# A two-layer graph kernel: one sum per feed-forward unit, and twelve sums of features, moved between ScalarE, GpSimd and VectorE

## The chip, the cores and the metric

The kernel runs on one core of one Trainium2 chip. The metric is the device time of one launch in microseconds (us), taken from repeated runs of the same program. Beside it stands a profile of one execution, which names what each engine did and when. The engines are called as the profile calls them: PE is TensorE (the matrix multiplier; PEld is its weight load), DVE is VectorE, ACT is ScalarE, POOL is GpSimd, and SP is SyncE, which here only issues transfers. Every engine works through its own list of instructions strictly in order; where one needs the result of another engine, it waits for a semaphore, and everything behind it in the same list waits too.

## The reference, cut to what matters

The input is 128 graphs of 128 nodes with 256 features each, and an integer adjacency matrix per graph. Two layers follow one another. All of it is float32.

```python
# layer 0: graph attention twice, then a feed-forward network
h = _gat(x, adj, W1, a1);  h = _gat(h, adj, W2, a2)     # softmax over masked scores
h = _layernorm(x + h, g_ln1, b_ln1)
x = _layernorm(h + relu(h @ w_ff1 + b_ff1) @ w_ff2 + b_ff2, g_ln2, b_ln2)

# layer 1: 8-head attention with 4 relations, then a feed-forward network
attn = softmax(q @ k.T / sqrt(32))
out  = sum over r of (attn * (adj == r)) @ (x @ Wv[r])
x = _ln(x + out @ Wo, g1, beta1)
x = _ln(x + gelu(x @ W1 + b1) @ W2 + b2, g2, beta2)
```

The change touches the first product of each feed-forward network, `h @ w_ff1` and `x @ W1`: for a group of 4 graphs it is a 512 x 256 matrix times a 256 x 1024 matrix.

## The kernel before

The graphs are worked through in 32 groups of 4. For each group there are stages (loading, graph attention, feed-forward of layer 0, multi-head attention, feed-forward of layer 1), written as Python generators. A small scheduler in the kernel interleaves the stages of neighbouring groups by planned times; for most of the kernel it also pins the order in which PE and SP get their instructions. The order on DVE, ACT and POOL comes out of the compiler's own scheduling, and it is fixed when the program is built.

The feed-forward product is done by a scheme of the Strassen kind: both matrices are cut into 2 x 2 blocks, and 7 block products and some sums of blocks take the place of 8 products. The sums of the weights are made once. The sums of the features are made once for each group and layer:

```python
def moving_sums(hT):                                        # line 279
    b11, b21, b12, b22 = ...                                # four blocks of the transposed features
    t1, t2, t4 = ...                                        # tiles of 128 x 256
    nc.gpsimd.tensor_sub(t1, b12, b11)                      # L283
    nc.gpsimd.tensor_sub(t2, b22, t1)                       # L284
    nc.gpsimd.tensor_sub(b12, b22, b12)                     # L285
    nc.gpsimd.tensor_sub(t4, t2, b21)                       # L286
    return None, b11, b21, b22, t4, t1, t2, b12
```

The results are made in two units for each group and layer, so there are 2 x 2 x 32 = 128 units in the kernel, and the two of one group take turns. One unit goes through four steps, and between the steps the other unit and other stages have their turn:

```python
def unit(f0):
    # lo, hi: two tiles of 128 x 2 x 2 x 256 in SBUF
    def product(p, k, first=False):                         # two matmuls of 256 columns
        for i in range(2):
            nc.tensor.matmul(p[:, i], win[k][...], hs[k], start=first and i == 0, stop=True, ...)  # L307

    chain, side = (ps.tile([P, 2, T // 2], F32, name="mm") for _ in range(2))   # PSUM
    product(chain, 1, True)
    product(side, 5, True)
    nc.scalar.copy(lo[:, :, 0], chain)                      # L313
    nc.scalar.copy(hi[:, :, 0], side)                       # L314
    yield
    p = ps.tile([P, 2, T // 2], F32, name="mm")
    product(chain, 6)
    product(p, 2, True)
    product(side, 3)
    nc.scalar.copy(lo[:, :, 1], chain)                      # L320
    nc.vector.tensor_add(lo[:, :, 0], lo[:, :, 0], p)       # L321
    nc.vector.tensor_add(lo[:, :, 1], lo[:, :, 1], side)    # L322
    yield
    product(chain, 7)
    nc.scalar.copy(hi[:, :, 1], chain)                      # L325
    nc.gpsimd.tensor_add(hi[:, :, 1], hi[:, :, 1], hi[:, :, 0])   # L326
    for i in range(2):
        nc.scalar.activation(lo[:, i], lo[:, i], func, ...) # L328
    yield
    product(chain, 4)
    for h, p in enumerate((chain, hi[:, :, 1])):
        for i in range(2):
            nc.scalar.activation(hi[:, i, h], p[:, i], func, ...)  # L334
    yield
```

Note the two products on `chain` at the end. Product 7 is added to `chain`; then that state of `chain` must be read out before product 4 is added on top of it. So the matmuls of product 4 wait for whoever reads `chain` after product 7.

Other lines that matter below, by their numbers in the profile:

```python
nc.gpsimd.tensor_tensor(y[...], y[...], v[...], op)         # L245 affine: gain and offset of a layer norm
nc.scalar.activation(y[:, b], y[:, b], AF.Identity, ...)    # L239 layer norm
nc.tensor.transpose(...)   /   nc.scalar.copy, nc.vector.tensor_copy   # L256, L260, L258: features on PE
nc.vector.transpose(z, y)                                   # L262: features by way of transfers
nc.tensor.matmul(..., fT[f][...], wout[:, f], ...)          # L351: second product of the feed-forward
nc.vector.tensor_add(y[...], y[...], p)                     # L352: and its sum with the residual
nc.scalar.copy(wh[...], p)                                  # L407, after the matmuls L406 (graph attention)
nc.tensor.matmul(scores...)                                 # L450
nc.vector.scalar_tensor_tensor(m, ab, r, eT, ...)           # L476: mask of one relation, four of them per graph
nc.tensor.matmul(p, hT..., wv...)  /  nc.vector.tensor_add(v..., p, bv)   # L483, L484: values
nc.tensor.matmul(po..., v..., ms[r]...)                     # L495: attention times values
```

PSUM holds six tiles named `mm` in turn for nearly all matmuls. The features reach their transposed form in two ways: for most groups by a DVE transpose of blocks and two transfers through DRAM, but for the first and the last group (`direct`) by PE, because nothing else could hide the transfers there.

Of the kernel before, what the change touches and what calls it, by code (L numbers as in the profile page):

```python
# [57 lines left out]
def graph_layers(ctx: ExitStack, tc: tile.TileContext, a: dict, out: bass.AP):  # L58
# [8 lines left out]
    nc = tc.nc  # L67
# [156 lines left out]
    def normalised(y, first=0, n=G):  # L224

        y = y[:, first:first + n]
        mv = sm.tile([P, n, 2], F32, name="mv")
        for b in range(n):
            st = sm.tile([P, 6], F32, name="st")
            nc.vector.bn_stats(st, y[:, b])  # L230
            nc.vector.bn_aggr(mv[:, b], st)
        rstd = sm.tile([P, n], F32, name="rstd")
        nc.gpsimd.tensor_scalar(rstd, mv[:, :, 1], EPS, None, op0=OP.add)
        nmr = sm.tile([P, n], F32, name="nmr")
        nc.gpsimd.tensor_scalar(nmr, mv[:, :, 0], -1.0, None, op0=OP.mult)
        nc.gpsimd.tensor_tensor(rstd, rstd, mhalf[:, :n], OP.pow)
        nc.gpsimd.tensor_mul(nmr, nmr, rstd)  # L237
        for b in range(n):
            nc.scalar.activation(y[:, b], y[:, b], AF.Identity, bias=nmr[:, b:b + 1], scale=rstd[:, b:b + 1])  # L239

    def affine(y, k, b, n, engine=nc.gpsimd):


        for op, v in zip((OP.mult, OP.add), ln[k]):
            engine.tensor_tensor(y[:, b:b + n], y[:, b:b + n], v[:, None, :].to_broadcast([P, n, D]), op)  # L245
# [26 lines left out]
    def features(y, direct):  # L272

        t = t_tile().rearrange("p (b c n) -> p b c n", b=G, c=DC)
        blocks = t.rearrange("p b c n -> p (b c) n")
        transposed(y.rearrange("p b (c f) -> p (b c) f", f=P), blocks, direct, blocks)
        return t

    def moving_sums(hT):

        b11, b21, b12, b22 = (hT[:, h:h + G // 2, c] for h in (0, G // 2) for c in range(DC))
        t1, t2, t4 = (wk.tile([P, G // 2, N], F32, name=f"t{i}") for i in (1, 2, 4))
        nc.gpsimd.tensor_sub(t1, b12, b11)  # L283
        nc.gpsimd.tensor_sub(t2, b22, t1)  # L284
        nc.gpsimd.tensor_sub(b12, b22, b12)  # L285
        nc.gpsimd.tensor_sub(t4, t2, b21)  # L286
        return None, b11, b21, b22, t4, t1, t2, b12

    def feed_forward(y, before, direct, win, bin_, wout, func, by=G):


        hT = features(y, direct)
        yield TIMES["lead ff0" if before == "01" else "lead ff1"]
        hs = moving_sums(hT)
        yield TIMES["sums"]
        fT = [None] * FC

        def unit(f0):

            lo, hi = (wk.tile([P, 2, 2, T // 2], F32, name="fT", bufs=FC // 2) for _ in range(2))  # L300
            for i in range(2):
                fT[f0 + i] = lo[:, i].rearrange("p h t -> p (h t)")
                fT[FC // 2 + f0 + i] = hi[:, i].rearrange("p h t -> p (h t)")

            def product(p, k, first=False):
                for i in range(2):
                    nc.tensor.matmul(p[:, i], win[k][:, ts(f0 + i, P)], hs[k], start=first and i == 0, stop=True,  # L307
                                     skip_group_check=True)

            chain, side = (ps.tile([P, 2, T // 2], F32, name="mm") for _ in range(2))  # L310
            product(chain, 1, True)
            product(side, 5, True)
            nc.scalar.copy(lo[:, :, 0], chain)  # L313
            nc.scalar.copy(hi[:, :, 0], side)  # L314
            yield
            p = ps.tile([P, 2, T // 2], F32, name="mm")
            product(chain, 6)
# [4 lines that stand above are left out]
            nc.vector.tensor_add(lo[:, :, 1], lo[:, :, 1], side)  # L322
            yield
            product(chain, 7)
            nc.scalar.copy(hi[:, :, 1], chain)  # L325
            nc.gpsimd.tensor_add(hi[:, :, 1], hi[:, :, 1], hi[:, :, 0])  # L326
            for i in range(2):
                nc.scalar.activation(lo[:, i], lo[:, i], func, bias=bin_[:, f0 + i:f0 + i + 1])  # L328
            yield
# [3 lines that stand above are left out]
                    f = FC // 2 + f0 + i  # L333
                    nc.scalar.activation(hi[:, i, h], p[:, i], func, bias=bin_[:, f:f + 1])  # L334
            yield

        units = [unit(0), unit(2)]
        for n, now in enumerate(((0,), (1,), (0,), (1,), (0,), (1,), (0,), (1,))):
            for u in now:
                next(units[u])  # L340
            if n in (2, 4):
                affine(y, before, n - 2, 2)
            yield TIMES["ff unit"]
        yield TIMES["ff2"]

        late = sorted(range(FC), key=lambda f: f % (FC // 2) // 2)
        for b2_ in range(0, G, 2):
            p = ps.tile([P, 2, D], F32, name="mm")
            for b in (b2_, b2_ + 1):
                for n, f in enumerate(late):  # L350
                    nc.tensor.matmul(p[:, b - b2_], fT[f][:, ts(b, N)], wout[:, f], start=n == 0, stop=n == FC - 1)  # L351
            nc.vector.tensor_add(y[:, b2_:b2_ + 2], y[:, b2_:b2_ + 2], p)  # L352
            yield TIMES["ff half"]
            if (b2_ + 2) % by == 0:
                normalised(y, b2_ + 2 - by, by)
        return y
# [185 lines left out]
    def ff0(y, direct):  # L542
        return feed_forward(y, "01", direct, wf1, bf1, wf2, AF.Relu)

    def ff1(y, direct, by):
        return feed_forward(y, "11", direct, later["w1"], b1, w2, AF.Gelu, by)
# [123 lines left out]
```

## Time and profile before

| quantity | value |
|---|---|
| time, median of 3 runs | 3191.92 us (3191.85 to 3194.92) |
| span of the profiled execution | 3190.1 us |
| PE matmul busy, PE weight load busy | 98%, 75% of the span |
| DVE, ACT, POOL busy | 61%, 55%, 48% of the span |
| L325, ScalarE copy 128 x 512 out of PSUM | 128 times, mean 578 ns |
| L326, GpSimd addition 128 x 512 in SBUF | 128 times, mean 1273 ns |
| L322, VectorE addition 128 x 512, one input in PSUM | 128 times, mean 676 ns |
| L283 to L286, GpSimd sums 128 x 256 | 64 times each, mean 726 or 727 ns |
| PE busy from 300 to 2900 us | 2597.68 of 2600 us |
| PE busy from 0 to 300 us, and from 2900 to 3190 us | 259.30 us, and 265.38 of 290 us |

The profile is read like this. The first part gives the busy time of each engine; the second cuts the span into 40 slices and gives the busy share of each in tenths. The groups of instructions put together all executions of one source line and give their mean, and the time for which their engine stood idle just before them, with the event that ended the idle time. The timeline lists single instructions with their start, their length and the same note on idle time. Matmuls overlap one another, so the length of a PE group in the timeline is a little longer than the time to the next group's start; the starts are the safe figure.

### The profile page before, as it was taken

To read this page: it belongs to the slowest core of one execution; us is meant where nothing else is said; L and a number is where in the kernel's file an instruction comes from. 1 tells how busy PE (TensorE), PEld (TensorE's weight loads), DVE (VectorE), ACT (ScalarE), POOL (GpSimd) and SP (SyncE) were. 2 spreads that over 40 slices of the span, in tenths; PEclk is the share of its full clock that TensorE was granted. 3 is DMA by queue.
4 is the path that set the end of the run, shared out by engine and by line. 5 is a ranking of instruction groups with operands and counts; after the bars stand their busy time and mean duration, and the time that the engine had idled before them with its cause. 6 is when DMAs were issued, how large, how long until landed. Compare 5 with 4: busy or idle time off the path is not lost.

```text
span 3190.1 us, 55111 instructions
## 1 busy us (share of the span) xinstructions
PE 3122.4 (98%) x20160; PEld 2379.2 (75%) x20160; DVE 1945.5 (61%) x3538; ACT 1745.1 (55%) x5191; POOL 1535.8 (48%) x1866
## 2 busy tenths in 40 slices
PE   7989999999999999999999999999999999999988
PEld 6756778777777777777777778777778777777766
DVE  3565566566566566566566566566566566566552
ACT  4435555565555565555565555565555565555543
POOL 3424455454455454455454455454455454455443
PEclk9999999999999999999999999999999999999999
DMA  4244454544453444454544454544454544453310
GB/s 164 60 92 104 107 117 96 119 91 102 106 122 92 117 83 111 107 117 96 119 87 107 107 121 94 117 92 101 107 118 96 119 93 101 105 123 89 78 34 14
DMA packets 1156398, 320.81 MB, mean 101 GB/s; under 512 B 902944, under 2 KB 1126688, under 8 KB 1156000
## 3 DMA queue, kind: packets, MB, share of 16 engines
q1 hardware_dynamic: 1156128, 317.29, 43.7%
q8 instruction: 160, 2.62, 0.3%
q14 instruction: 110, 0.90, 0.1%
HBM read 187.58 MB, written 129.62 MB: 99 GB/s over the span
## 4 chain that ended last, share of the span: by engine, by line
PE 84%; DMA 5%; DVE 5%; ACT 2%; SPq 2%; POOL 1%; issue 1%; ACTq 0%; DVEq 0%; POOLq 0%
PE mm L351 25%; PE mm L307 21%; PE mm L483 11%; PE av L495 6%; PE mm L450 4%; PE mm L398 3%; PE mm L436 3%; PE mm L430 3%; PE mm L533 3%; DVE m L476 2%; DMA eT<-zd 2%; DMA zd<-e 2%; PE mm L416 2%; PE mm L406 2%; SPq L265 1%
## 5 line engine op out<-in xcount | busy, mean ns | idle before, releaser
L476 DVE SCALAR_TENSOR_TENSOR m<-adj,eT 128x1024 f32<-128x1024 f32 x512 | 598.7, 1213 | 199.1 <-DMA eT<-zd 189.5
L245 POOL TENSOR_TENSOR tok<-tok,ln_rows 128x512 f32<-128x512 f32 (+1 forms) x636 | 671.0, 1062 | 41.0 <-PE mm L256 15.3
L462 POOL TENSOR_TENSOR e<-e,s 128x512 f32<-128x512 f32 x256 | 266.6, 1042 | 565.3 <-DVE s L461 548.3
L460 ACT ACTIVATE e<-mm,nm 128x128 f32<-128x128 f32 x1024 | 360.0, 375 | 210.0 <-DVE nm L456 206.6
L483 PE MATMUL mm<-wv,T 128*128 128x512 f32 x1024 | 465.8, 598 | 0.2 <-ACT e L460 0.2
L351 PE MATMUL mm<-wf,fT 128*128 128x256 f32 x2048 | 456.8, 381 | 0.6 <-ACT fT L334 0.6
L351 PE MATMUL mm<-w,fT 128*128 128x256 f32 x2048 | 455.5, 381 | 0.0
L351 PEld LDWEIGHTS mm<-w,fT 128*128 128x128 f32 x2048 | 387.1, 190 | 73.7 <-issue 23.5
L351 PEld LDWEIGHTS mm<-wf,fT 128*128 128x128 f32 x2048 | 386.9, 190 | 63.5 <-ACT fT L334 8.9
L483 PEld LDWEIGHTS mm<-wv,T 128*128 128x128 f32 x1024 | 192.3, 191 | 201.2 <-issue 194.7
L387 POOL TENSOR_TENSOR e<-e,s 128x512 f32<-128x512 f32 (+1 forms) x68 | 67.2, 989 | 501.6 <-DVE s L386 408.8
L239 ACT ACTIVATE tok<-tok,nmr,rstd 128x256 f32<-128x256 f32 x512 | 268.8, 593 | 72.4 <-POOL nmr L237 72.4
L495 PE MATMUL av<-m,v 128*32 128x128 f32 x8192 | 254.5, 276 | 7.6 <-DVE m L476 4.5
L495 PEld LDWEIGHTS av<-m,v 128*32 128x32 f32 x8192 | 217.9, 110 | 54.2 <-issue 40.5
L352 DVE TENSOR_TENSOR tok<-tok,mm 128x512 f32<-128x512 f32 x128 | 86.8, 678 | 261.7 <-PE mm L351 261.5
L326 POOL TENSOR_TENSOR fT<-fT 128x512 f32<-128x512 f32 x128 | 161.6, 1273 | 146.0 <-ACT fT L325 146.0
L460 ACT ACTIVATION_READ_ACCUMULATOR e<-mm,nm 128x1 f32 x1024 | 219.5, 214 | 0.0
L484 DVE TENSOR_TENSOR v<-mm,bv 128x512 f32<-128x512 f32 x256 | 169.8, 684 | 79.4 <-PE mm L483 79.4
L374 ACT ACTIVATE e<-e,wh 128x128 f32<-128x128 f32 x240 | 77.8, 411 | 247.5 <-DMA e<-zsd 247.5
L456 DVE TENSOR_REDUCE nm<-mm 128x4 f32<-128x512 f32 x256 | 162.7, 675 | 59.7 <-PE mm L450 59.7
L307 PE MATMUL mm<-T,w 128*128 128x256 f32 x768 | 196.6, 386 | 0.2 <-ACT T L260 0.2
L307 PE MATMUL mm<-T,wf 128*128 128x256 f32 x768 | 193.8, 382 | 0.1
(124 smaller groups left out, 5137.7 us busy)
## 6 DMA issues: line engine op xcount, KB each, us to landing
zd<-e SPq DMA_DIRECT2D x496, 128.0 KB, 3.1
eT<-zd SPq DMA_DIRECT2D x124, 512.0 KB, 4.0
zd<-T SPq DMA_DIRECT2D x364, 128.0 KB, 3.6
T<-zd SPq DMA_DIRECT2D x91, 512.0 KB, 4.1
xt<-in_xT_dram SPq DMA_DIRECT2D x32, 512.0 KB
at<-in_adjT_dram SPq DMA_DIRECT2D x64, 256.0 KB, 6.3
tok<-in_x_dram SPq DMA_DIRECT2D x32, 512.0 KB
out_dram<-tok SPq DMA_DIRECT2D x31, 512.0 KB, 6.6
```

The lines of the kernel that those rows point to most:

```text
L239: nc.scalar.activation(y[:, b], y[:, b], AF.Identity, bias=nmr[:, b:b + 1], scale=rstd[:, b:b + 1])
L245: engine.tensor_tensor(y[:, b:b + n], y[:, b:b + n], v[:, None, :].to_broadcast([P, n, D]), op)
L307: nc.tensor.matmul(p[:, i], win[k][:, ts(f0 + i, P)], hs[k], start=first and i == 0, stop=True, skip_group_check=True)
L326: nc.gpsimd.tensor_add(hi[:, :, 1], hi[:, :, 1], hi[:, :, 0])
L351: nc.tensor.matmul(p[:, b - b2_], fT[f][:, ts(b, N)], wout[:, f], start=n == 0, stop=n == FC - 1)
L456: nc.vector.tensor_reduce(nm, p, AX.X, OP.max, negate=True)
L460: nc.scalar.activation(eh[:, q], p[:, q], AF.Exp, bias=nm[:, q:q + 1], accum_out=s[:, q:q + 1])
L462: nc.gpsimd.tensor_mul(eh, eh, per_row(s, N))
L476: nc.vector.scalar_tensor_tensor(m, ab, r, eT, op0=OP.is_equal, op1=OP.mult)
L483: nc.tensor.matmul(p, hT[:, b, f], wv[:, f, r:r + 2], start=f == 0, stop=f == DC - 1)
L484: nc.vector.tensor_add(v[:, r:r + 2].rearrange("p r d -> p (r d)"), p.rearrange("p r d -> p (r d)"), bv[:, r * D:(r + 2) * D])
L495: last = nc.tensor.matmul(po[ts(q, DH), c], v[:, r, c * P + q * DH:c * P + (q + 1) * DH], ms[r][:, q // 2 * HC + c * 2 + q % 2], start=r = ...
```

## The change

The change does two things.

First, in each unit the sum that closes `hi[:, :, 1]` is made by one VectorE addition which reads `chain` in PSUM directly. The ScalarE copy of `chain` and the GpSimd addition fall away. For that, the copy of `side` goes into `hi[:, :, 1]` at once, where the sum is wanted, and not into `hi[:, :, 0]`. This is meant to take a long and slow pair of instructions out of ScalarE and GpSimd and to shorten the path from product 7 to the activation.

Second, the four sums of features are made by VectorE where the features come directly from PE: in layer 0 for the first and the last group, and in layer 1 for the last group. That is 3 times 4 instructions. All other groups keep GpSimd.

```diff
-    def moving_sums(hT):
+    def moving_sums(hT, engine):
         ...
-        nc.gpsimd.tensor_sub(t1, b12, b11)
-        nc.gpsimd.tensor_sub(t2, b22, t1)
-        nc.gpsimd.tensor_sub(b12, b22, b12)
-        nc.gpsimd.tensor_sub(t4, t2, b21)
+        engine.tensor_sub(t1, b12, b11)
+        engine.tensor_sub(t2, b22, t1)
+        engine.tensor_sub(b12, b22, b12)
+        engine.tensor_sub(t4, t2, b21)
         ...
-        hs = moving_sums(hT)
+        hs = moving_sums(hT, nc.vector if direct else nc.gpsimd)
         ...
             nc.scalar.copy(lo[:, :, 0], chain)
-            nc.scalar.copy(hi[:, :, 0], side)
+            nc.scalar.copy(hi[:, :, 1], side)
         ...
             product(chain, 7)
-            nc.scalar.copy(hi[:, :, 1], chain)
-            nc.gpsimd.tensor_add(hi[:, :, 1], hi[:, :, 1], hi[:, :, 0])
+            nc.vector.tensor_add(hi[:, :, 1], hi[:, :, 1], chain)
```

No matmul is added or taken away, and no transfer. Lines of the changed kernel behind this place have numbers smaller by one.

## The prediction

> **What bounds the kernel now.** I read the page's busy shares first, then its slices, then the waits of PE in three stretches, and last the timeline where the changed instructions stand.
>
> ```profile
> PE 3122.4 (98%) x20160; PEld 2379.2 (75%) x20160; DVE 1945.5 (61%) x3538; ACT 1745.1 (55%) x5191; POOL 1535.8 (48%) x1866
> PE   7989999999999999999999999999999999999988
> PEclk9999999999999999999999999999999999999999
> PE 84%; DMA 5%; DVE 5%; ACT 2%; SPq 2%; POOL 1%; issue 1%; ACTq 0%; DVEq 0%; POOLq 0%
> ```
>
> The busy share alone would not convince me, but the slices show full PE from the fourth slice to nearly the last, and the chain that ended last is 84% PE. Asked for the waits of PE between 300 and 2900 us, the trace names two, 1.2 us together; PE is busy 2597.68 of those 2600 us. Equal places of neighbouring groups (product 4 of layer 0 at 1566.39 and 1661.80 us) are 95.41 us apart. So in the middle **PE is the bound and has no gap**: time freed on ACT or POOL is worth nothing there, and any wait that the change puts into PE's list is paid in full, once per group. Only the first 300 us (259.30 busy) and the last 290 (265.38 busy) have idle PE to win.
>
> The place that decides is the third and fourth step of the units in layer 0. These rows of the timeline repeat in each group:
>
> ```profile
> 1656.58 4.61 DVE L476 SCALAR_TENSOR_TENSOR m<-adj,eT 128x1024 f32<-128x1024 f32 x4
> 1656.64 1.89 PE L307 MATMUL mm<-T,wf 128*128 128x256 f32 x8
> 1657.70 0.58 ACT L325 COPY fT<-mm 128x512 f32<-128x512 f32 x1 [0.66 <-PE mm L307]
> ...
> 1658.36 3.60 PE L483 MATMUL mm<-wv,T 128*128 128x512 f32 x8
> ...
> 1661.11 0.68 DVE L322 TENSOR_TENSOR fT<-fT,mm 128x512 f32<-128x512 f32 x1
> ...
> 1661.70 1.28 DVE L484 TENSOR_TENSOR v<-mm,bv 128x512 f32<-128x512 f32 x2
> 1661.80 1.89 PE L307 MATMUL mm<-t,wf 128*128 128x256 f32 x8
> ```
>
> PE does product 7 of both units (1656.64), then L483, then product 4 of both (1661.80), without a gap. Before, ACT reads `chain` in between (L325) and is long done. DVE spends that time on four masks (L476), does L322 until 1661.79, and then the two value additions L484.
>
> **What the Trainium skill says.** "PSUM — Partial Sum Buffer", section "The four PSUM rules": GpSimd cannot touch PSUM. That is why the old sum needs a ScalarE copy first; the trace agrees, L326 has only SBUF tiles. "SBUF — State Buffer", section "Who interferes with whom": a VectorE instruction with two SBUF inputs contends with a GpSimd one that reads SBUF, and the later one waits; with one SBUF input, outside the two-port modes, it does not. The trace agrees for L381 (two SBUF inputs, 512 elements): 0.69 us at 1586.25, but 1.13 us at 1647.95, while L245 ran on POOL until 1648.53. So the new unit addition (one input in PSUM) should be as quick as L322, and the sums of features may be held up by L245. "TensorE: Matmul & The Clock Gate", section "What's actually happening": an idle PE falls to half clock until it has been busy for a while. The trace agrees in kind, though a wait of about 2 us is already enough: after 2.05 us at 3029.58, four matmul instructions of 256 columns took 1.92 us where 1.03 is usual; after 1.20 us at 156.46 nothing slowed.
>
> **The change part by part.**
>
> *Removed:* 128 copies L325 x 0.578 = 74 us of ACT, 128 additions L326 x 1.273 = 163 us of POOL, and 12 sums x 0.727 = 9 us of POOL. Neither engine is the bound: worth nothing by itself.
>
> *Added:* 128 VectorE additions. By L322's row (676 ns) that is 87 us, DVE 61% to 64%. Twelve sums of 256 elements, about 0.4 us each (L534, 256 elements: 408 ns), more where L245 runs.
>
> *The middle.* I read the order of instructions of the changed kernel as it is built. PE's list between the ends is unchanged, and so are the transfers. On DVE, in 28 groups of layer 0, the order is: four L476, L322, **both new additions, then** the two L484. DVE does not run ahead here, because the L321 before the masks waits for PE itself (start 1655.97, idle 0.30 before). So the first new addition ends at 1661.79 + 0.59 (the pitch from L322 to the next addition, 1661.11 to 1661.70) = 1662.38. PE starts about 0.06 us after a DVE release (at 199.96; the first of two L484 from 199.22, 0.68 long, ended at 199.90). Product 4 then starts at 1662.44 and not 1661.80: **0.64 us** of wait. The second addition ends at 1662.98, before PE has done the 0.86 us of the first unit: no further wait. I took the same difference in all 28 groups: in most, L322 ends 0.01 us before product 4; in five it ends 0.13 to 0.45 after, which adds 1.4 us. 28 x 0.64 + 1.4 = 19.3, and 0.4 for the last group: **+20 us**. A second, smaller wait may follow. ACT's built order now has both runs of L239, the rest of L328 and all L334 ahead of L407. From POOL's release of the second L239 (about 1661.5 without one L326) I add ACT's pitches: 1.98 + 1.24 + 1.60 + 1.42 gives 1667.9 for the freeing of the second `chain`; L450 would want a PSUM tile at 1667.88. A tenth of a microsecond per group: **+2 us**, uncertain.
>
> In layer 1 there is no such wait: the additions stand behind a DVE transpose which ends 3.5 us before product 4, so 2.8 to 3.0 us remain in every group there.
>
> *The end.*
>
> ```profile
> 3148.28 3.71 POOL L245 TENSOR_TENSOR tok<-tok,ln_rows 128x512 f32<-128x512 f32 x3 [11.35 <-PE mm L256]
> ...
> 3149.19 0.67 DVE L258 COPY T<-mm 128x512 f32<-128x512 f32 x1
> ...
> 3151.95 0.72 POOL L283 TENSOR_TENSOR t<-T 128x256 f32<-128x256 f32 x1
> ...
> 3152.72 1.25 PE L307 MATMUL mm<-t,w1s 128*128 128x256 f32 x4 [2.79 <-POOL t L283]
> ```
>
> The features are there at 3149.86, but the first sum waits behind three L245 on POOL. On DVE it can begin at about 3150.0 and be done at 3150.4 to 3151: PE gains some 2.0 us. After this wait, 44 matmul instructions took 11.45 us in the chain; at 0.216 each (32 in 6.91) they need 9.5. With a short wait that slow clock should not come: 1.7 us more. At the very end an affine L245 on DVE (3179.96) stands before the last L352 (3180.57), though PE is done at 3179.74; in the new order it stands behind: 1.2 us. Together **-5 us**.
>
> *The start.* PE waits 1.21 us for L283 at 59.83, 0.56 for L334 at 78.85, 1.20 for a mask at 156.46 and 1.20 for L484 at 199.96. New orders on DVE favour all four (reciprocals no longer behind waiting masks), but one new addition at about 112 us delays two L321 by 0.6 us. I count 3 of the 4.2: **-3 us**.
>
> Sum: 3191.9 + 20 + 2 - 5 - 3 = 3206. I shade it to **3203** for the rivals.
>
> **Rivals.** (1) *The wait does not come*, because DVE is earlier than I think or PE has hidden slack; then only the ends count: 3184. For it: the change takes two instructions off this very path and puts one in their place. Against: the 0.01 us margin and the unbroken PE. About one in five. (2) *DVE becomes a wider bound*: L484 and the copies behind it come 1.2 us later in each group, and a PSUM tile or a mask is late elsewhere too, another 0.5 us in 29 groups: 3220. Against: DVE at 64%, and L495 wants L484 only at 1665.36, when its shifted end is about 1664.2. One in seven. (3) *Relief of ACT and POOL shortens the middle*: PE's two waits there sum to 1.2 us, and spacings above 95.41 add 6 us over 27 groups; at best 3178. One in twenty-five.
>
> **Range and chances.** The range runs from rival 1, 3184, to most of rival 2, 3217. The bounds at 2% are 3128 and 3256: the idle PE at the two ends, 65 us, could hold a gain so large only if nearly all of it went, and a loss so large needs 2.2 us per group. Within 2%: 0.975.
>
> **What would show it.** In the changed kernel's PE waits from 300 to 2900 us, a row of L307 waiting for the new addition, some 28 times at 0.6 to 0.7 us; groups spaced about 96.1 us; PE busy there below 2590. At the end, no wait of 2.79 us at the first sum, and normal-speed matmuls after it. ACT near 1671 us busy, POOL near 1364, DVE near 2040. I am wrong if the spacing stays 95.4 (first step of the middle), if waits of L450 or L351 for ACT exceed 0.3 us per group (second step), or if the head loses time by its changed DVE order.

## The result and the profile after

The changed kernel takes 3210.36 us (median of 4 runs, 3210.16 to 3213.03), the kernel before 3191.89 us in the same measurement: the ratio is 1.0058, 95% interval 1.004 to 1.0075. So the change makes the kernel slower by about 18.5 us, well within 2%. The prediction said 3203, range 3184 to 3217.

In the changed kernel the new VectorE addition is L325, the masks are L475, the values L482 and L483, attention times values L494. The page:

```profile
PE 3123.2 (97%) x20160; PEld 2376.0 (74%) x20160; DVE 2028.7 (63%) x3678; ACT 1689.5 (53%) x5063; POOL 1371.4 (43%) x1726
PE   7979999999999999999999999999999999999998
```

PE has the same work in a span that is 18.3 us longer. Its slices are as full as before. ACT, POOL and DVE are busy for 1689.5, 1371.4 and 2028.7 us, where the prediction had 1671, 1364 and 2040; that only shows that the work went where it was sent. The waits of PE between 300 and 2920 us (the columns are total, times, longest) name one row:

```profile
PE mm L307 <- DVE fT L325: 16.9, 27, 1.3
```

The timeline shows one of these waits. These are the same instructions of the same group that the prediction showed, 9.63 us later on the clock:

```profile
1666.21 4.61 DVE L475 SCALAR_TENSOR_TENSOR m<-adj,eT 128x1024 f32<-128x1024 f32 x4
1666.27 1.89 PE L307 MATMUL mm<-T,wf 128*128 128x256 f32 x8
...
1670.74 0.68 DVE L322 TENSOR_TENSOR fT<-fT,mm 128x512 f32<-128x512 f32 x1
...
1671.33 1.28 DVE L325 TENSOR_TENSOR fT<-fT,mm 128x512 f32<-128x512 f32 x2
...
1672.16 1.96 PE L307 MATMUL mm<-t,wf 128*128 128x256 f32 x8 [0.57 <-DVE fT L325]
```

Product 7 and the masks start 0.06 us apart, as before. Where the first value addition used to follow L322, the two unit additions now stand. The first ends at about 1672.01, PE starts product 4 at 1672.16. From the start of product 7 to that of product 4 it is 5.89 us, where it was 5.16: 0.73 us of wait.

To see where the 18.3 us went, I cut each profiled span at the starts of product 4 in layer 0, which are the safest marks: the head up to the first of them past 300 us, 27 distances between groups, and the rest. In the head I also give the time from the first weighting in the second graph attention of the first group (the matmuls L415, L416 in the kernel before, with `wh` and `e`, that start at 42 to 46 us), because the loading stage ahead of them varied by 3.5 us between these profiles, though no list of instructions differs there.

| kernel | head from launch | from first weighting | 27 distances | median distance | rest |
|---|---|---|---|---|---|
| before | 321.5 | 277.2 | 2582.2 | 95.43 | 286.5 |
| after | 323.2 | 280.4 | 2600.4 | 96.27 | 284.8 |
| difference | +1.8 | +3.2 | **+18.2** | +0.84 | -1.7 |

### The profile page after: what moved, and what is told of

It reads as the page before. It is cut to its first block, busy times and chain, and to the rows that moved or that the text cites. A ratio compares the mean times of both kernels' runs of the same rounds, so it can differ in the third digit from the quotient of the medians.

```text
span 3208.4 us, 55193 instructions
## 1 busy us (share of the span) xinstructions
PE 3123.2 (97%) x20160; PEld 2376.0 (74%) x20160; DVE 2028.7 (63%) x3678; ACT 1689.5 (53%) x5063; POOL 1371.4 (43%) x1726
## 4 chain that ended last, share of the span: by engine, by line
PE 57%; DVE 4%; DMA 1%; issue 0%; ACT 0%; SPq 0%; POOL 0%; ACTq 0%; POOLq 0%; DVEq 0%
PE mm L350 18%; PE mm L307 15%; PE mm L482 7%; PE av L494 5%; DVE m L475 3%; PE mm L449 3%; PE mm L532 2%; PE mm L435 2%; PE mm L429 2%; PE mm L397 2%; PE mm L405 1%; PE mm L415 1%; DVE fT L325 0%; DVE fT L322 0%; DMA eT<-zd 0%
## 5 line engine op out<-in xcount | busy, mean ns | idle before, releaser
L475 DVE SCALAR_TENSOR_TENSOR m<-adj,eT 128x1024 f32<-128x1024 f32 x512 | 598.8, 1213 | 239.0 <-DMA eT<-zd 176.7
L245 POOL TENSOR_TENSOR tok<-tok,ln_rows 128x512 f32<-128x512 f32 (+1 forms) x636 | 669.3, 1061 | 41.7 <-PE mm L256 15.1
L482 PE MATMUL mm<-wv,T 128*128 128x512 f32 x1024 | 465.2, 597 | 0.0
L350 PE MATMUL mm<-wf,fT 128*128 128x256 f32 x2048 | 457.1, 381 | 0.0
L350 PE MATMUL mm<-w,fT 128*128 128x256 f32 x2048 | 455.5, 381 | 0.9 <-DVE v L483 0.9
L350 PEld LDWEIGHTS mm<-w,fT 128*128 128x128 f32 x2048 | 386.6, 190 | 75.4 <-issue 23.8
L350 PEld LDWEIGHTS mm<-wf,fT 128*128 128x128 f32 x2048 | 386.4, 190 | 63.3 <-ACT wh L406 8.6
L239 ACT ACTIVATE tok<-tok,nmr,rstd 128x256 f32<-128x256 f32 x512 | 269.3, 594 | 137.7 <-POOL nmr L237 125.1
L482 PEld LDWEIGHTS mm<-wv,T 128*128 128x128 f32 x1024 | 192.1, 190 | 200.6 <-issue 192.1
L494 PE MATMUL av<-m,v 128*32 128x128 f32 x8192 | 258.3, 278 | 15.2 <-DVE v L483 11.2
L494 PEld LDWEIGHTS av<-m,v 128*32 128x32 f32 x8192 | 220.7, 111 | 62.1 <-issue 43.6
L283 POOL TENSOR_TENSOR t<-T 128x256 f32<-128x256 f32 x61 | 44.5, 730 | 479.5 <-DMA T<-zd 479.5
L483 DVE TENSOR_TENSOR v<-mm,bv 128x512 f32<-128x512 f32 x256 | 167.6, 684 | 49.3 <-PE mm L482 49.3
L230 DVE BATCH_NORM_STATS2 st<-tok 128x6 f32<-128x256 f32 x512 | 187.0, 413 | 0.6
```

What stands on the lines that cost most here:

```text
L475: nc.vector.scalar_tensor_tensor(m, ab, r, eT, op0=OP.is_equal, op1=OP.mult)
L482: nc.tensor.matmul(p, hT[:, b, f], wv[:, f, r:r + 2], start=f == 0, stop=f == DC - 1)
L483: nc.vector.tensor_add(v[:, r:r + 2].rearrange("p r d -> p (r d)"), p.rearrange("p r d -> p (r d)"), bv[:, r * D:(r + 2) * D])
L494: last = nc.tensor.matmul(po[ts(q, DH), c], v[:, r, c * P + q * DH:c * P + (q + 1) * DH], ms[r][:, q // 2 * HC + c * 2 + q % 2], start=r = ...
```

## The experiments

All ratios are to the kernel before, run beside it on the same chip, with the 95% interval. The medians of the kernel before lie between 3191.89 and 3198.23 us in these measurements, so ratios of different experiments are compared here to no better than 0.2%. The other figures come from one profile per kernel. Three kernels with the same lists of instructions in the middle (the kernel before, the one with the sums alone, and the one with the last group's sums alone) took 2582.2, 2583.0 and 2585.2 us for the 27 distances; a difference of less than 3 us in that column shows nothing. Line numbers shift a little from kernel to kernel.

### One half of the change at a time

The change without its unit additions:

```diff
-            nc.vector.tensor_add(hi[:, :, 1], hi[:, :, 1], chain)
+            nc.scalar.copy(hi[:, :, 1], chain)
+            nc.gpsimd.tensor_add(hi[:, :, 1], hi[:, :, 1], hi[:, :, 0])   # and `side` into hi[:, :, 0]
```

> The sums of features of the first and last groups go to VectorE; the units keep the ScalarE copy and the GpSimd addition. Theory (the middle pays for the unit addition, the head pays for a new VectorE order that comes with the sums of the first group): groups 95.4 us apart as before and no wait for the unit addition; near 240 us PE waits 8 to 9 us for the second value addition, as in the changed kernel; at the end no wait of 2.8 us at the first sum, worth about 3 us. In all about 3193 us (3188 to 3198). Rival (the loss at the head comes from the 128 new additions on VectorE): no such wait at 240 us, and only the gain at the end: about 3187 us.

Measured: 1.0004 (0.9995 to 1.0013), 3195.8 against 3194.2 us. Head from the first weighting 280.2, distances 2583.0 in all, rest 284.3. A wait of 9.26 us for the second value addition stands at 249 us. The middle is untouched, the end gains 2.2 us (about 3 were expected), the head loses 3.0.

The change without its sums:

```diff
-        hs = moving_sums(hT, nc.vector if direct else nc.gpsimd)
+        hs = moving_sums(hT, nc.gpsimd)
```

> The unit addition goes to VectorE; all sums stay on GpSimd. Theory: groups 96.26 us apart, PE waits for the unit addition some 27 times at 0.6 us by the trace, together +18 us in the middle (+23 by the spacing, less 5 us by which short stalls in layer 1 go away); at 240 us no wait of 8 us; the first sum at the end still waits 2.8 us. In all about 3204 us (3199 to 3209). Rival (head loss from the additions): the 8 us wait at 240 us is there and the total is 3212 us or more.

Measured: 1.0034 (1.0022 to 1.0046). Head from the first weighting 272.1, distances 2600.6, rest 287.0. PE waits for the unit addition 28 times, 16.7 us; no wait of 8 us at 240 us. So the middle belongs to the unit additions, and the loss in the head to the sums, as the theory said. Alone, the unit additions even gain 5.1 us in the head, which was not expected. The two halves don't add up there: -5.1 and +3.0 make +3.2 together, so the sums cost 3.0 without the additions and 8.3 with them.

### The middle: is it the place in the list, or VectorE's load?

The same instructions, with one thing changed: a dependency puts the third mask of the set, and with it the fourth, behind the two additions. The build then also moved ScalarE's second run of L239 and two VectorE additions further behind in each group.

```diff
             nc.vector.tensor_add(hi[:, :, 1], hi[:, :, 1], chain)
+            added[0] = nc.cur_bb.bb.instructions[-1]
...
             by_relation(0, eT[0], ms, PARTS[k // 2:k // 2 + 1])
+            if k == 4 and 0 < g < NG - 1:
+                tc.add_manual_dep(nc.cur_bb.bb.instructions[-1], added[0].name, ...)   # order only
```

> The changed kernel with one thing altered: in layer 0 the third and fourth mask of the first set stand behind the two unit additions on VectorE, where they stood ahead. The same instructions, the order of the other engines but for ScalarE unchanged. Theory (the wait comes from the place in VectorE's list, behind four masks of 1.15 us each): the wait of product 4 vanishes in all groups, spacing 95.4 us, 23 us less: about 3187 us (3184 to 3192), the head as in the changed kernel. Rival (VectorE's load is what makes PE wait): the wait comes back at the value addition, the masks or the scores behind, spacing stays near 96.2, about 3208 us.

Measured: 0.998 (0.9973 to 0.9988). The distances sum to 2577.2 us, median 95.41. First the only row of PE's waits from 300 to 2920 us, then the timeline, where L478 are the masks, L327 the additions, L309 the products:

```profile
PE mm L538 <- DVE v L486: 0.2, 1, 0.2
```

```profile
1657.65 2.35 DVE L478 SCALAR_TENSOR_TENSOR m<-adj,eT 128x1024 f32<-128x1024 f32 x2
1657.71 1.89 PE L309 MATMUL mm<-T,wf 128*128 128x256 f32 x8
...
1660.51 1.27 DVE L327 TENSOR_TENSOR fT<-fT,mm 128x512 f32<-128x512 f32 x2
1661.70 2.35 DVE L478 SCALAR_TENSOR_TENSOR m<-adj,eT 128x1024 f32<-128x1024 f32 x2
1662.87 1.89 PE L309 MATMUL mm<-t,wf 128*128 128x256 f32 x8
```

The additions end at 1661.8, a microsecond ahead of product 4, which starts 5.16 us after product 7 again. VectorE does the same work in the middle, and what stands behind it holds PE for 0.2 us in all. That settles it: the 23 us between the two kernels come from two masks of 1.15 us standing ahead of the additions instead of behind.

The opposite experiment puts one more VectorE instruction into the same place, a copy whose result is written over later:

```diff
+            if before == "01" and f0 == 0:
+                nc.vector.tensor_copy(hi[:, :, 0], chain)
             nc.vector.tensor_add(hi[:, :, 1], hi[:, :, 1], chain)
```

> The changed kernel with one more VectorE instruction ahead of the first unit's addition in layer 0: a copy of `chain` into a part of the tile that is written over later (an added instruction; the output stays what it was). Theory (each VectorE instruction between the masks and product 4 is paid by PE in full, once per group): the wait grows by one pitch, 0.59 us, spacing 96.85 us, 28 x 0.59 = 16.5 us over the changed kernel. Rival (PE has slack elsewhere in the group that takes up a part): spacing grows by less than 0.4 us, under 11 us in all.

Measured: 1.0104 (1.009 to 1.0118). The row of PE's waits from 300 to 2930 us, where L327 is the unit addition:

```profile
PE mm L307 <- DVE fT L327: 32.8, 27, 1.6
```

The wait goes from 16.9 to 32.8 us, the median distance to 96.81, the 27 distances to 2615.3: +14.9 us, 0.55 us per group for a copy whose pitch is 0.60 us. PE pays for practically all of it, as the theory said; the rival's 0.4 us is excluded.

The third experiment keeps the additions in layer 1 alone, and the sums in the last group alone:

```diff
+        new = before == "11"       # layer 1: the addition as changed; layer 0: copy and GpSimd addition
...
-        hs = moving_sums(hT, nc.vector if direct else nc.gpsimd)
+        hs = moving_sums(hT, nc.vector if late_sums else nc.gpsimd)    # the last group only
```

> The new unit addition in layer 1 only (layer 0 keeps the ScalarE copy and the GpSimd addition), and the sums on VectorE in the last group only. Theory: in layer 1 the addition lies 3 us ahead of product 4, so no wait comes; the old stalls of 0.3 us at product 4 of layer 1, where the ScalarE copy stood behind a table load, go away (5 us in all, spacing 95.4 in every group); the end gains 3 to 4 us; the head stays as before. About 3183 us (3180 to 3187). Rival (any addition put on VectorE makes PE wait, for VectorE is the wider bound): spacing above 95.7 us, 3195 us or more.

Measured: 0.9978 (0.997 to 0.9986). The head stays (276.9 from the first weighting), the distances sum to 2578.7, 3.5 us under the kernel before, the rest is 284.3, a gain of 2.2 where 3 to 4 were expected. All four kernels here that have the addition in layer 1 and no wait in layer 0 lie between 2576.7 and 2578.7, under the three of 2582.2 to 2585.2. So the addition does bring something, in layer 1. What it takes away there is a stall that the view of waits didn't list. In the kernel before, one of the groups that have it:

```profile
748.66 1.28 ACT L328 ACT_TABLE_LOAD   x1
...
749.95 2.56 ACT L328 ACTIVATE fT<-fT,col 128x512 f32<-128x512 f32 x4
...
752.67 1.06 ACT L325 COPY fT<-mm 128x512 f32<-128x512 f32 x2
...
753.39 1.10 PE L307 MATMUL mm<-t,w 128*128 128x256 f32 x4
```

The same place in the changed kernel:

```profile
757.12 0.35 ACT L498 COPY oT<-av 128x256 f32<-128x256 f32 x1
757.37 1.70 ACT L333 ACTIVATE fT<-fT,col 128x256 f32<-128x256 f32 x4
...
758.25 1.03 PE L307 MATMUL mm<-t,w 128*128 128x256 f32 x4
```

Before, ScalarE loads the table for Gelu, then does four activations and a copy for the attention, and only then reads `chain` (L325). Product 4 starts 0.3 us late. Put over one another, 11 of the 27 groups of the kernel before show this stall of 0.16 to 0.30 us, 3.0 us in all, and none of the changed one.

### The end

Only the line with `late_sums` of the last diff is changed: the sums of the last group on VectorE, and no unit addition.

> The kernel before with one thing altered: the sums of the last group alone on VectorE; the first group's sums and all unit additions as before. Theory: head and middle as before, no wait of 2.8 us at the first sum of the end but one of 1.2 us, matmul at usual speed behind it, the affine step still ahead of the last half: 2.2 to 3 us under the kernel before, 0.999. Rival (the slow matmul and the sums on VectorE come from elsewhere or are given back by VectorE's sums beside GpSimd's affine): no gain at the end.

Measured: 0.9989 (0.9981 to 0.9998). The rest takes 284.3 us instead of 286.5: 2.2 us, and the first sum's wait is 1.17 instead of 2.79, as expected. In the changed kernel:

```profile
3170.53 3.90 POOL L245 TENSOR_TENSOR tok<-tok,ln_rows 128x512 f32<-128x512 f32 x3 [11.35 <-PE mm L256]
...
3172.22 1.08 DVE L283 TENSOR_TENSOR t<-T 128x256 f32<-128x256 f32 x1
...
3173.36 1.13 PE L307 MATMUL mm<-t,w1s 128*128 128x256 f32 x4 [1.17 <-DVE t L283]
...
3174.64 0.41 DVE L285 TENSOR_TENSOR T<-T 128x256 f32<-128x256 f32 x1
```

L283 takes 1.08 us and L284 1.37 us while GpSimd's L245 runs until 3174.43; L285 and L286, which start when no L245 runs, take 0.41 us each. The Trainium skill, "SBUF — State Buffer", section "Who interferes with whom", says that a VectorE instruction with two SBUF inputs contends with a GpSimd one that reads SBUF; this trace agrees. Behind the four matmuls after the short wait (1.13 us) the next four take the usual 1.03. After 2.79 us of wait the first four took 1.25 us and the next 1.92 in the kernel before, and the first four 2.07 in the one with the additions alone.

### The head: 9 us of wait, but not 9 us of loss

The changed kernel near 240 us, VectorE's list and the PE instruction that waits for it:

```profile
233.89 0.66 DVE L483 TENSOR_TENSOR v<-mm,bv 128x512 f32<-128x512 f32 x1
...
240.90 0.18 DVE L460 RECIPROCAL s<-s 128x4 f32<-128x4 f32 x1 [6.36 <-ACT e L459]
...
242.67 0.68 DVE L483 TENSOR_TENSOR v<-mm,bv 128x512 f32<-128x512 f32 x1
...
243.40 3.64 PE L494 MATMUL av<-m,v 128*32 128x128 f32 x64 [8.90 <-DVE v L483]
```

In the kernel before:

```profile
239.62 1.28 DVE L484 TENSOR_TENSOR v<-mm,bv 128x512 f32<-128x512 f32 x2
...
240.96 1.96 PE L495 MATMUL av<-m,v 128*32 128x128 f32 x64 [0.57 <-DVE v L484]
```

There both value additions stood ahead of that reciprocal, and PE waited 0.57 us. Now the second stands behind it and waits with it for ScalarE's exponentials. The wait costs more than itself: the 64 matmuls behind it take 3.64 us where they took 1.96, at a granted clock of 0.50 from 236.94 to 247.18 us. I put this place back as it was:

```diff
+            if g == 1 and b == 1:      # the reciprocal of the next graph and the capping L380: behind the value additions
+                tc.add_manual_dep(turns[2], summed[0], ...)
```

> The changed kernel with one place of VectorE's list put back as it was before, near 240 us: the second value addition of the second group stands ahead of the reciprocal and the capping that wait for ScalarE, where the change had put it behind them. Theory (the head's loss is that one order): PE's wait of 8.9 us for this value addition shrinks to about 1 us, product 4 of the first full group (323 us) comes 5 to 8 us earlier, and the middle keeps its spacing of 96.3: 5 to 8 us under the changed kernel. Rival (the sums of the first group on VectorE cost the head by their own time, and the order is a symptom): another wait takes its place, under 2 us.

Measured: 1.0049 (1.0034 to 1.0064), head from the first weighting 278.0: by the profile 2.4 us gained, not 5 to 8, and by the ratios, 1.0049 against 1.0058, no gain that can be told from noise. The wait is 1.79 us, but PE then waits 2.67 us for exponentials, and 3.32 us at 259 us for a token addition that stands behind two masks. So I moved those masks too:

```diff
+                if g == 1 and b == 2 and r == 0:
+                    behind("mask")      # this mask behind both token additions L416 of the group after next
```

> The previous cure of the head brought less than half of what the wait of 8.9 us promised, and its trace shows a second place of the same kind at 256 us: a token addition stands in VectorE's list behind two masks that wait for a transfer, and PE waits 3.3 us for it. Here those masks stand behind both token additions as well. Theory (the head's loss is a chain of places in VectorE's list, each with its own wait): the 3.3 us wait goes, and from the first weighting product (about 44 us) to the first product 4 of the full groups (about 323 us) it takes 274 to 276 us, against 278.0 with one cure, 280.4 without and 272.1 with the sums on GpSimd. Rival (something else in the head holds PE, and waits only move): 277.5 us or more.

Measured: 1.0034 (1.0021 to 1.0047), head 279.7. By this profile the theory fell: the wait for L416 went, and one of 3.98 us for another addition came (261 us), with 4.13 us for exponentials. Moving single instructions moved the waits. The runs leave this less certain: the profile is of the slowest of five (3211.19 us, median 3207.83), and the ratio is lower than the changed kernel's, though the intervals overlap. The last experiment therefore tests the order as a whole. The four sums of the first group stay on VectorE, and the lists of PE, VectorE, ScalarE and GpSimd up to 320 us are held to the order that they have with these sums on GpSimd:

```diff
+HELD = {PE: [...800 indices], DVE: [...300], Activation: [...380], Pool: [...110]}
...
+    for engine, indices in HELD.items():
+        chain = [traced[k] for k in indices if traced[k].engine == engine]
+        for i, previous in zip(chain[1:], chain):
+            tc.add_manual_dep(i, previous.name, ...)
```

> The changed kernel, its sums of the first group on VectorE, but with the lists of PE, VectorE, ScalarE and GpSimd held, up to about 320 us, to the order that they have when these sums are on GpSimd (the order of the kernel with the unit additions alone). So the four VectorE sums at 58 us run as in the changed kernel, and the order of all that follows is the one that took 272.1 us from the first weighting product to the first product 4 of the full groups, where the changed kernel took 280.4. Theory (the head is lost by the order that the build chose, not by the sums): 271 to 273.5 us there, the wait of 8.9 us gone, and about 8 us under the changed kernel in all. Rival (the four sums on VectorE cost the time themselves, or what they contend with): 277 us or more there, no gain.

Measured: 1.0017 (1.001 to 1.0024), clear of the changed kernel's interval; span 3201.2 us, head from the first weighting 271.6. In the head the sums themselves cost nothing; the order that came with them costs the 8.3 us. Cut once more, at the matmul L415 of the fourth group (248 to 254 us), one sees what the single cures did:

| kernel | first weighting to L415 | L415 to product 4 |
|---|---|---|
| before | 209.8 | 67.4 |
| after | 208.9 | 71.6 |
| additions alone | 204.3 | 67.8 |
| value addition moved | 203.5 | 74.5 |
| and the masks moved | 204.5 | 75.1 |
| order held | 203.6 | 68.0 |

Moving the value addition won all of the first part (5.4 us) and gave 2.9 back in the second, where VectorE's list had been rearranged with it. It also shows why a wait of 8.9 us was worth only 5: with the additions alone, where that wait is 1.02 us, PE stands 6.46 us before L415, for a softmax whose scores come by transfer. Which of the instructions in the second part costs the 3.8 us there I have not separated.

### Versions that beat both kernels

The edit of the masks in the middle and that of the value addition in the head, together:

> Both cures together: in layer 0 the unit additions ahead of the third and fourth mask, and near 240 us the value addition ahead of the waiting reciprocal. Theory: the two effects add: spacing 95.4 us, the wait at 240 us about 1 us, 28 to 31 us under the changed kernel, 0.994 to 0.996 of the kernel before. Rival (the head's cure is eaten up by the wait of the second group's next stage): as with the unit additions alone, 0.998.

Measured: 0.9965 (0.9952 to 0.9977). Head 276.5 from the first weighting, distances 2576.7: the middle's cure came in full, the head's again in part.

The edit of the masks in the middle, and `late_sums`:

> The unit additions on VectorE ahead of the third and fourth mask in layer 0, and the sums on VectorE in the last group only, so that the first groups keep VectorE's old order. Theory: head as with the additions alone (product 4 at about 317 us), spacing 95.4 us and no 0.3 us stalls in layer 1 (middle 2577 us), the end as in the changed kernel (284 us): 316.7 + 2577.3 + 284 = 3178 us by the profile, some 0.995 of the kernel before. Rival (the head's gain of the additions needs the masks' old place): head at 321 us or more, 0.997.

Measured: **0.9952** (0.994 to 0.9965), 3179.5 against 3194.1 us. Head 271.0 from the first weighting, distances 2577.7, rest 283.9, each as expected. By the midpoints it is the fastest of all kernels here.

## Why the prediction was right, and where it was not

The total was 7 us low: 3 of these came from shading 3206 to 3203, the rest from the parts. The middle was forecast 3.8 us too dear, the end 3.3 and the start 4.8 us too cheap; errors cancelled. That the middle came so close is luck in part too, for there the wait was taken too small and a gain beside it was left out.

- **"PE is the bound and has no gap"** in the middle: right for what matters, as the doubled wait and the additions ahead of the masks show. But not quite without a gap. The 27 distances of the kernel before sum to 6.1 us over 27 x 95.41. The view of waits listed 1.2 of it, two waits for value additions; the 11 stalls behind the table load are 3.0 more. With the additions ahead of the masks only 1.2 us over 27 x 95.41 are left.
- **"0.64 us of wait"**, 28 times, +20: the mechanism was right to the instruction, the size too small. Each group pays 0.85 us (96.26 against 95.41). The wait itself is 0.73: I took 0.06 us from the addition's end to PE's start, from another release, and here it was 0.15. Of the other 0.12, after the wait the eight matmuls of product 4 take 0.07 us longer (1.96 against 1.89), and 0.05 more is lost at the scores, by the next point. So 27 x 0.85 = 23.0, plus 1.3 in the groups where VectorE comes later (I had 1.4), less the 6.1 above: 18.2, as measured.
- **"+2 us" for a second wait of L450 for ScalarE**: it came, at about half the size, though PE's list of waits doesn't show it. The scores of the kernel before, then of the changed one, where L449 is what was L450:

  ```profile
  1667.24 1.13 PE L450 MATMUL mm<-kbd,T 64*128 64x256 f32 x8
  ```

  ```profile
  1676.14 1.54 ACT L333 ACTIVATE fT<-mm,col 128x256 f32<-128x256 f32 x4
  ...
  1677.67 0.78 PEld L449 LDWEIGHTS mm<-kbd,T 64*128 64x128 f32 x8 [0.20 <-ACT fT L333]
  1677.68 1.18 PE L449 MATMUL mm<-kbd,T 64*128 64x256 f32 x8
  ```

  ScalarE is done with the second `chain` at 1677.68, the very moment at which the scores begin; their second matmul starts 0.05 us late, and the eight take 1.18 us instead of 1.13. In 21 of the 27 groups this adds up to 0.9 us. (The 0.20 us is idle time of the weight load that stands there in the kernel before too.) With the additions ahead of the masks, and with the doubled wait, it doesn't come, and so the copy of 0.60 us cost only 0.55. That the forecast came near is luck: the pitches as written add up to 1667.7 and not 1667.9, before the 1667.88 at which L450 would want the tile.
- **"-5 us" at the end**: three terms against new waits. The first sum gave 1.6, not 2.0, because L283 took 1.08 us beside L245, the upper end of the 0.4 to 1 us that I had allowed. The slow clock gave its 1.7: from the waiting product to L350 it takes 9.60 us, where it took 11.29. The affine step's new place gave 0.6 of 1.2 (last matmul to the end of the span: 9.7 and 10.4 us). Against these 3.9 us stand 1.06 us of the unit addition's wait in the last group and 0.91 us of L350 for a value addition (2986 us), neither of which the end of the kernel before had. I had put only 0.4 down for the last group. Measured: -1.7.
- **"-3 us" at the start**: this failed. I took four waits from the page, asked whether the new order favours them, and added. Three of them went, 3.0 us. The fourth, for the first sum, stayed (1.18 us at 58.21, where it was 1.21). By 206 us the changed kernel was even 7.7 us ahead on the clock, of which 1.4 came from the loading. Then the rest of the order took more than that back. I had counted waits up to 200 us and nothing in the next 120, although "the head loses time by its changed DVE order" stood among what would make me wrong.
- **Rivals**: the first (no wait) and the second (VectorE as a wider bound) are excluded by doubling the wait and by moving the additions. The third (relief shortens the middle) was treated as an alternative to the wait, with one chance in twenty-five. It came as well as the wait: -4.9 us in the kernel with the additions ahead of the masks. Effects that don't exclude one another belong in the sum, not among the rivals.

## What to carry to other kernels

Where one engine is the bound, ask of each instruction that moves to another engine not how long it takes but what stands ahead of it in that engine's list when its input is ready; here 0.68 us of addition cost 0.85 us per group behind four masks and nothing behind two. Measure a saturated stretch by the distance of equal marks, for the stalls of up to 0.3 us here were in no list of waits. And where a scheduler fixes the order, moving four instructions to another engine can rearrange the lists of four engines behind them, here from 59 to 284 us: hold the order, or leave the stretch as it was, before putting the result down to the instructions themselves.

## What the runs showed of the hardware

A PE that has waited 0.57 us loses more than the wait, at a granted clock of 1.00: the next eight matmuls of 256 columns took 1.96 us where 1.89 is usual. After a wait of 1.17 us the clock stayed at 1.00 as well, in the changed kernel at 3173.36 us. After 2.79 us it fell to 0.50 for 3.41 us: from 3153.61 us in the kernel before, 0.89 us after the matmuls had begun again, and from 3167.55 us, 0.09 us before they began, in the kernel with the additions alone. From the end of a VectorE addition to the start of the PE matmul that it releases I measured 0.06 us in one place and 0.15 us in another.
